# Three score tiles and a single bank for bites in late attention; experts' tiles in pairs with shared array rows

## The chip, the cores and the metric

The kernel runs on one core of one Trainium2 chip, as one program that computes a whole transformer block. The metric is the device time of one execution in microseconds. The program has in-order engines that run side by side: PE (TensorE, with PEld for its weight loads), ACT (ScalarE), DVE (VectorE), POOL (GpSimd), and SP (SyncE), which issues most DMAs. Matrix products land in PSUM, which has eight banks of 128 x 512 float32. Everything here is float32. A float32 matmul shows as two PE instructions, and a transpose against the identity as one.

## The reference

The input is x[4, 1024, 256]; every position t of the second axis has four rows, one for each l.

```
x = x + attention(layernorm(x))     # 16 heads of 16, rotary, per-head layernorm of q and k,
                                    # scores ** 4, causal mask, divided by their sum, then w_out
x = x + ffn(layernorm(x))
x = x + conv(layernorm(x))          # a convolution over the first axis (4 taps), then silu
x = x + ffn(layernorm(x))

def ffn(x):                         # 4096 rows of 256
    shared = silu(x @ s1_gate) * (x @ s1_up) @ s2          # width 352
    probs = softmax(x @ gate_w.T)                          # 16 experts
    weights, chosen = top_k(probs, 6)
    for each row and each chosen expert e:
        h = silu(x @ w1[e]_gate) * (x @ w1[e]_up)          # width 176
        out += weight * (h @ w2[e])                        # 176 x 256
    return out + shared
```

The hidden width of an expert, 176, is 128 + 48, so the contraction of the second matmul (the down projection) takes two weight loads of at most 128 rows.

## The kernel before

**Attention.** A pass is half hf of the 1024 positions, times a pair u (one of four l and one of two groups of heads): eight passes with hf = 0 (early) and eight with hf = 1 (late). A step (n, a, j) of a pass handles one block j of 128 keys for four heads. An early pass has 2 x 4 steps and a late one 2 x 8, so there are 64 early and 128 late steps. `forward` calls `scores`, two steps ahead (LOOK = 2): four matmuls of 32 contraction rows each (L694), one for each head, into two score tiles of 128 x 2 x 512 (two banks each); ACT squares both from PSUM (L705); then masks (DVE L712, POOL L714); then the second square, of tile 0 on DVE (L725), of tile 1 on ACT (L863, in the next turn of the loop) or in part on POOL. `weigh` (L742) multiplies with v into the one accumulator bank. PSUM there: a pool of two score tiles (four banks), one accumulator, three banks for everything else ("m").

That everything else is cut into bites: generators that yield "pe", "el" or "gap", in five lanes of the class `Bites`: QKV0, QKV1 (projection, rotary, norms and transposes of a coming pass: `qkv_bites`, started by `begin_chain`), NORM, OUT (collecting a pass's output and projecting it), and ROUTE (taps, zero fill of the queues xq, then for the first half of the rows the router: `prepare`, `plan`, `scatter`). `bites.step(pe, counts)` runs up to counts[lane] bites of each lane in the order of the lanes, and at most pe bites of kind "pe" over all of them. There are two such calls in a step. `plan` computes the slots of all rows in queues sorted by expert, and a table of the expert of each of 111 tiles of 128 slots. `scatter` normalizes two 128-row blocks into a buffer sxn (two buffers, DVE L200) and sends them to xq in DRAM with 12 indirect DMAs from POOL (L421), 96 in all.

The order of instructions on PE, DVE, ACT and SP is the order of the program text; POOL's is the compiler's.

**Feed-forward.** `stream` runs 4 stages of 111 tiles: stage 0 and 2 for the first and second feed-forward of the first half of the rows, 1 and 3 for the other half. Iteration c does `load` (SP, three tiles a DMA, xg), `gate_up(c)` (L1030, weights picked by a register; Silu on ACT L1038, product on DVE L1039 into hbuf), `turn_h(c - 2)` (two transposes of hbuf, L1044, copied by ACT to hT), `turn(c + 2)` (two transposes of the tile's input, L1014), `down(c - 3)` (L1053: hT's first 128 rows with w2a and the rest, 48 rows padded with zeros to 128, with w2b; copied by ACT to yo, stored by SP to yq for every third tile), and then the stage's own function, which runs bites in three lanes: QUEUE (`combine` of the stage before: gathers from yq by indirect DMAs on POOL, L1147, added into X on DVE, L1131; then `fill`, the scatter for the stage after), SIDE (`convolve`, `prepare`, `plan`) and FILL (`shared`, the shared expert: L955, L972). If the next stage's queue is not filled six tiles before it is wanted, `force` runs what is left of the lanes at once. After the last tile the rest of `combine` runs with `shared` of the last half.

All weights of the experts lie in SBUF: wgu, w2a, and w2b with all 16 experts.

## Time and profile before

| | |
|---|---|
| median of 3 runs | 2390.59 us (2389.18 to 2391.22) |
| the profiled execution | 2393.24 us, its span 2391.5 us |
| busy, PE / PEld | 2114.5 us (88%) / 1308.4 us (55%) |
| busy, DVE / ACT / POOL | 1118.5 / 1240.2 / 901.4 us (47, 52, 38%) |
| mean granted PE clock | 0.925 |
| early attention; late attention | to 275.2 us; 275.2 to 760 us |
| first gate_up of stages 0 to 3 | 854.8, 1168.9, 1570.8, 1977.0 us |
| last gate_up; end | 2253.7 us; 2391.5 us |
| scatters, gathers on POOL (L421, L1147) | 384 x 0.987 us, 384 x 0.979 us |
| chain that ended last, by engine | PE 67%, DVE 12%, issue 7%, ACT 7%, POOL 5%, DMA 2% |

Matmuls are pipelined and their ends are modelled, so a busy PE is read by the distances between starts. In a line of the timeline the columns are start, duration, engine, line, operation, out<-in, shape and count, and in brackets the idle time of the engine just before and what ended it. Idle time of an engine that does not set the end costs nothing.

### The profile page before, as it was taken

What the parts mean: (1) busy time and instruction counts of PE and PEld (TensorE: products, weight loads), DVE (VectorE), ACT (ScalarE), POOL (GpSimd) and SP (SyncE); (2) the same over time, 40 slices, a digit from 0 to 9 for tenths busy, and PEclk for the clock granted to TensorE, in tenths of its full rate; (3) what the DMA queues carried; (4) which work ended last, traced back from release to release, by engine and by line L of the source; (5) the groups of instructions that cost most, each with busy time, mean ns of one, the idle gap of its engine ahead of it and who ended that gap; (6) DMA issues with size and microseconds to landing.
All of it is one profiled execution on the core that took longest, in us unless ns stands there. A gap on an engine that the chain in (4) does not pass through costs nothing.

```text
span 2391.5 us, 33033 instructions
## 1 busy us (share of the span) xinstructions
PE 2114.5 (88%) x10480; PEld 1308.4 (55%) x10480; DVE 1118.5 (47%) x2532; ACT 1240.2 (52%) x2754; POOL 901.4 (38%) x990
## 2 busy tenths in 40 slices
PE   5899999778898998999899999789999959999974
PEld 2344443222233466777666667567676747777632
DVE  5888867656555225111166652126754212441154
ACT  3677878566676145555455544335553424555410
POOL 3333211344431000444355226645513654540176
PEclk8888988889888999999999999989999979999987
DMA  7900000111101412555455335344423535663243
GB/s 232 342 7 1 1 1 1 38 51 45 53 27 62 114 48 79 165 166 166 137 151 154 102 104 176 132 139 142 145 92 121 176 124 154 202 186 115 91 123 112
DMA packets 212231, 267.73 MB, mean 112 GB/s; under 512 B 25280, under 2 KB 187232, under 8 KB 212064
## 3 DMA queue, kind: packets, MB, share of 16 engines
q1 hardware_dynamic: 166944, 161.04, 21.6%
q0 software_dynamic: 36992, 100.78, 13.4%
q10 hardware_dynamic: 8128, 3.80, 0.7%
q8 instruction: 91, 1.49, 0.3%
q14 instruction: 76, 0.62, 0.1%
HBM read 123.72 MB, written 141.82 MB: 111 GB/s over the span
## 4 chain that ended last, share of the span: by engine, by line
PE 67%; DVE 12%; issue 7%; ACT 7%; POOL 5%; DMA 2%; ACTq 0%; POOLq 0%; DVEq 0%; SPq 0%
PE pgu L1030 20%; PE py L1053 14%; PE ps L694 6%; PE acc L742 4%; PE pxt L1014 4%; PE pht L1044 4%; POOL xq L421 3%; PE pg L955 3%; ACT s L705 3%; PE pj L571 3%; PE pu L955 3%; PE po L972 3%; POOL yg L1147 2%; ACT s L863 1%; DVE X L1131 1%
## 5 line engine op out<-in xcount | busy, mean ns | idle before, releaser
L421 POOL DMA_INDIRECT xq<-sxn,sloti x384 | 379.2, 987 | 644.7 <-ACT xgT L1016 306.2
L1030 PE MATMUL pgu<-wgu,xgT 128*128 x1776 | 609.7, 466 | 4.4 <-DVE hbuf L1039 2.2
L1147 POOL DMA_INDIRECT yg<-yq,sloti x384 | 375.8, 979 | 421.8 <-issue 201.4
L1039 DVE TENSOR_TENSOR hbuf<-hbuf,pgu 128x176 f32<-128x176 f32 x444 | 149.4, 337 | 721.7 <-ACT hbuf L1038 721.2
L1030 PEld LDWEIGHTS pgu<-wgu,xgT 128*128 128x128 f32 x1776 | 338.7, 193 | 136.5 <-issue 20.3
L1038 ACT ACTIVATE hbuf<-pgu 128x176 f32<-128x176 f32 x444 | 141.4, 318 | 411.7 <-PE pgu L1030 411.6
L705 ACT ACTIVATE s<-ps 128x1024 f32<-128x1024 f32 (+3 forms) x384 | 291.4, 815 | 114.6 <-PE ps L694 113.5
L1053 PE MATMUL py<-w2a,hT 128*128 x888 | 268.7, 385 | 0.9 <-ACT yo L1062 0.9
L1053 PE MATMUL py<-w2b,hT 128*128 x888 | 266.4, 382 | 0.0
L1062 ACT COPY yo<-py 128x256 f32<-128x256 f32 x444 | 166.1, 374 | 167.0 <-PE py L1053 166.7
L1131 DVE SCALAR_TENSOR_TENSOR X<-yg,top,X 128x256 f32<-128x256 f32 x384 | 186.0, 484 | 87.8 <-DMA yg<-yq,sloti 81.8
L1014 PE MATMUL pxt<-ident,xg 128*128 128x128 f32 x888 | 171.8, 276 | 60.6 <-DMA xg<-xq 60.6
L714 POOL TENSOR_SCALAR_AFFINE_SELECT s<-s 128x256 f32<-128x256 f32 x128 | 84.2, 659 | 349.7 <-ACT s L705 349.5
L725 DVE TENSOR_TENSOR s<-s 128x1024 f32<-128x1024 f32 (+3 forms) x160 | 168.2, 1051 | 86.8 <-ACT s L705 83.5
L1016 ACT COPY xgT<-pxt 128x256 f32<-128x256 f32 x444 | 167.9, 378 | 68.7 <-PE pxt L1014 68.3
L694 PE MATMUL ps<-q,kA 32*128 32x512 f32 (+3 forms) x1024 | 182.0, 647 | 20.0 <-ACT s L705 18.0
L1044 PEld LDWEIGHTS pht<-ident,hbuf 128*128 128x128 f32 x888 | 125.9, 142 | 124.4 <-issue 71.1
L1053 PEld LDWEIGHTS py<-w2b,hT 128*128 128x128 f32 x888 | 170.2, 192 | 23.5
L863 ACT ACTIVATE s<-s 128x1024 f32<-128x1024 f32 x192 | 164.4, 856 | 27.5 <-POOL s L714 27.2
L1044 PE MATMUL pht<-ident,hbuf 128*128 128x128 f32 x888 | 171.6, 275 | 4.9 <-ACT hT L1046 4.9
L1046 ACT COPY hT<-pht 128x256 f32<-128x256 f32 x444 | 165.4, 372 | 1.7 <-PE pxt L1014 0.7
L742 PE MATMUL acc<-s,vA 128*32 128x512 f32 (+3 forms) x1024 | 140.1, 603 | 13.2 <-ACT s L863 10.8
(158 smaller groups left out, 2421.9 us busy)
## 6 DMA issues: line engine op xcount, KB each, us to landing
xg<-xq SPq DMA_DIRECT2D x148, 384.0 KB, 3.7
yq<-yo SPq DMA_DIRECT2D x148, 384.0 KB, 2.8
xq<-zero SPq DMA_DIRECT2D x74, 384.0 KB, 4.6
xq<-sxn,sloti POOLq DMA_INDIRECT x384, 2.4
yg<-yq,sloti POOLq DMA_INDIRECT x384, 2.9
wgu<-in_w SPq DMA_DIRECT2D x4, 1408.0 KB, 17.8
X<-in_x SPq DMA_DIRECT2D x8, 512.0 KB, 5.5
out<-X SPq DMA_DIRECT2D x8, 512.0 KB, 3.5
```

Of the source, the lines that this page charges most:

```text
L421: d = nc.gpsimd.indirect_dma_start(out=xq[g][:, :], out_offset=bass.IndirectOffsetOnAxis(ap=sloti[:, c + i, k : k + 1], axis=0), in_=xs[:, ...
L694: nc.tensor.matmul(tiles[h // 2][:, h % 2, 0:nq], lhsT=kt[32 * h : 32 * h + 32, (j % 4) * P : (j % 4 + 1) * P], rhs=qT[u, hf][a][32 * h : ...
L705: nc.scalar.activation(s2[:, :, 0:nq], tiles[pr][:, :, 0:nq], AF.Square)
L725: nc.vector.tensor_mul(part, part, part)
L742: nc.tensor.matmul(acc[32 * r : 32 * r + 32, n0:512], lhsT=va[:, j % 4, h * VW : h * VW + 32], rhs=s2s[r // 2][:, r % 2, 0 : 512 - n0], st ...
L863: nc.scalar.activation(part, part, AF.Square)
L1014: nc.tensor.transpose(pt[:, k, :], xg[c][:, k * P : (k + 1) * P], ident)
L1030: nc.tensor.matmul(pg, lhsT=xT[c][:, k, :], rhs=wgu_f[k][:, bass.ds(vals[0] * (2 * FI), 2 * FI)], start=(k == 0), stop=(k == 1),)
L1044: nc.tensor.transpose(pt[:, k, :], hbuf[c % 4][:, k * P : (k + 1) * P], ident)
L1053: nc.tensor.matmul(py, lhsT=hT[c][:, k, :], rhs=w2_f[k][:, bass.ds(off[c] * E, E)], start=(k == 0), stop=(k == 1),)
L1131: nc.vector.scalar_tensor_tensor(X[:, t, l, :], yg[:, k, :], top[:, i, k0 + k : k0 + k + 1], X[:, t, l, :], op0=ALU.mult, op1=ALU.add,)
L1147: nc.gpsimd.indirect_dma_start(out=yg[:, k, :], out_offset=None, in_=yq[g][:, :], in_offset=bass.IndirectOffsetOnAxis(ap=sloti[:, i, k0 + ...
```

## The change

In attention the PSUM pools go. There are now three score tiles (six banks), one bank `sums` for the accumulator and one bank `spare`. Early passes use two score tiles and turn `spare` and the two banks of the third tile over to the bites; late passes use all three score tiles in turn, and their bites have `spare` alone and run "pe" bites only in the second `bites.step` of a step, one at most. In late passes DVE also takes the second square of tile 1 at j = 1 and 3. Chains of late passes begin two passes ahead (at a = 1, j = 6), with a third vB buffer.

In the stream, tiles go in pairs. The pair's hidden rows lie in one buffer of 3 x 128 columns, the even tile's 176 from the left, the odd tile's 176 from the right, so that the middle 128 columns hold the even tile's last 48 and the odd tile's first 48, and one transpose turns both. `down` runs once a pair: for each tile a matmul with 128 rows of its expert (w2a in two layouts), then for each a matmul with its half of the middle (64 rows of the array, with 48 that are not zero). The 48 rows of w2 for each tile are no longer held for all experts but fetched by SP with a DMA for each tile (`fetch`), by a register that SP loads from the table. yo is copied and stored once a pair.

The lanes run otherwise too: middle stages take 1 + i % 2 bites of QUEUE and 3 of SIDE an iteration (1 and 2 before); `final` takes one of QUEUE each time with two gathers a bite (every second time with three before); `combine` keeps three bites pending, in four buffers yg; `plan` compares in chunks of 19 tiles (six bites) instead of 37 (three).

The diff, cut to its core:

```diff
-        for c in range(0, NTILE, 37):
+        for c in range(0, NTILE, 19):
+            n = min(19, NTILE - c)
             yield "el"
...
-        vB = [v_buffer(f"vB{i}") for i in range(2)]
+        vB = [v_buffer(f"vB{i}") for i in range(3)]
...
+        score_tiles = [pp.tile([P, 2, 512], FP, name=f"sc{i}") for i in range(3)]
+        sums = pp.tile([P, 512], FP, name="sums")
+        spare = pp.tile([P, 512], FP, name="spare")
...
+        early = Banks([spare, score_tiles[2][:, 0, :], score_tiles[2][:, 1, :]])
+        late = Banks([spare])
+        PS = {"m": early}
+        turn = [0]
...
-            tiles = [PS["s"].tile([P, 2, 512], FP, tag="s", name="ps") for _ in range(2)]
+            tiles = []
+            for _ in range(2):
+                tiles.append(score_tiles[turn[0] % (2 if hf == 0 else 3)])
+                turn[0] += 1
...
-                if pr == 0 and (hf == 1 or j % 2 == 0):
+                if pr == 0 and (hf == 1 or j % 2 == 0) or hf == 1 and j in (1, 3):
                     nc.vector.tensor_mul(part, part, part)
...
-            if hf == 1 and u > 0 and a == 0 and j == 3 and n + 1 < len(passes):
-                begin_chain(n + 1)
+            if hf == 1 and a == 1 and j == 6 and n + 2 < len(passes):
+                begin_chain(n + 2)
+            if hf == 1:
+                PS["m"] = late
...
-                    bites.step(1, (1, 1, 1, 1, 1))
+                bites.step(0 if PS["m"] is late else 1, (1, 1, 1, 1, 1))
...
-        w2b = fw.tile([P, NEXP, E], FP, name="w2b")
-        nc.vector.memset(w2b[32:64], 0.0)
-        nc.vector.memset(w2b[64:P], 0.0)
-        nc.scalar.dma_start(out=w2b[0:FB], in_=w2r[P:FI])
+        w2a = []
+        for a in range(2):
+            w2a.append(fw.tile([P, NEXP, E], FP, name=f"w2a{a}"))
+            nc.scalar.dma_start(out=w2a[a], in_=w2r[a * FB : a * FB + P])
+        w2b = [fw.tile([P, E], FP, name=f"w2b{i}") for i in range(3)]
+        for w in w2b:
+            nc.vector.memset(w, 0.0)
...
+            def fetch(c):
+                _, vals = expert(c, SP)
+                if tiles[c][1] % 2 == 0:
+                    rows, src = slice(0, FB), bass.ds(vals[0] * FI + P, FB)
+                else:
+                    rows, src = slice(P - FB, P), bass.ds(vals[0] * FI, FB)
+                nc.sync.dma_start(out=w2b[nth_pair(c) % 3][rows, :], in_=w2[src, :])
...
             def turn_h(c):
                 pt = ps_t.tile([P, 2, P], FP, tag="t", name="pht")
-                for k in range(2):
-                    nc.tensor.transpose(pt[:, k, :], hbuf[c % 4][:, k * P : (k + 1) * P], ident)
+                c0 = 2 * P * (tiles[c][1] % 2)
+                nc.tensor.transpose(pt[:, 0, :], pair(c)[:, c0 : c0 + P], ident)
+                if ends_pair(c):
+                    nc.tensor.transpose(pt[:, 1, :], pair(c)[:, P : 2 * P], ident)
...
+                py = ps_y.tile([P, 2, 512], FP, name="py")
+                for a in range(n):
+                    nc.tensor.matmul(
+                        py[:, a, 0:E],
+                        lhsT=hT[c + 1 - n + a][:, 0, :],
+                        rhs=w2a_f[a][:, bass.ds(off[c + 1 - n + a] * E, E)],
+                        start=True,
+                        stop=False,
+                    )
+                for a in range(n):
+                    rows = slice(HP * a, HP * a + HP)
+                    nc.tensor.matmul(
+                        py[:, a, 0:E],
+                        lhsT=hT[c][rows, 1, :],
+                        rhs=w2b[nth_pair(c) % 3][rows, :],
+                        start=False,
+                        stop=True,
                     )
+                yo = f2.tile([P, 2, E], FP, name="yo")
+                nc.scalar.copy(yo[:, 0:n, :], py[:, 0:n, 0:E])
...
                 if c >= 3:
-                    down(c - 3)
+                    if ends_pair(c - 3):
+                        down(c - 3)
+                if c + 2 < n:
+                    fetch(c + 2)
...
-                    yg = f3.tile([P, n, E], FP, tag="yg", name="yg")
+                    yg = f4.tile([P, n, E], FP, tag="yg", name="yg")
...
-                    if len(pending) > 2:
+                    if len(pending) > 3:
...
-                bites.step(1, (1, 2, 0))
+                bites.step(1, (1 + i % 2, 3, 0))
...
-                bites.add(QUEUE, combine(0, 3, store))
-            bites.step(1, (1 if i % 2 == 0 else 0, 0, 0))
+                bites.add(QUEUE, combine(0, 2, store))
+            bites.step(1, (1, 0, 0))
...
-            bites.add(QUEUE, combine(1, 3, last))
+            bites.add(QUEUE, combine(1, 2, last))
```

`prepare` and `plan` in the stream take their PSUM from the two banks of `shared`, since `py` now takes two.

## The prediction

> **What bounds the kernel now.** I read the windows by stage first, then the chain of waits, then the timeline inside each stage. Late attention (the passes with hf = 1, 275 to 760 us) in the windows, then the waits in it (who waited for whom: total us, times, longest):
>
> ```profile
> 275.20:760.00 484.80, 416.20 (x2484) 146.06 (x2483) 297.56 (x535) 353.97 (x484) 148.97 (x173) 0.87 0.08 27
> ...
> PEld ps L694 <- ACT s L705: 111.5, 132, 2.1
> ...
> ACT s L705 <- PE ps L694: 79.9, 72, 3.3
> ...
> ACT s L863 <- POOL s L714: 27.2, 8, 8.3
> ```
>
> (The last line is from the same query over 440 to 765 us.) After the span the columns are PE, PEld, DVE, ACT, POOL, clock. Nothing is full: ACT works 354 of 485 us, and it waits 80 us for scores while the scores wait 111 us for ACT's squares: a ping-pong over two score tiles, at a clock of 0.87.
>
> The tile stream, one iteration of the timeline on PE, undisturbed:
>
> ```profile
> 1000.85 1.35 PE L1030 MATMUL pgu<-wgu,xgT 128*128 x4
> ...
> 1002.04 0.38 PE L1044 MATMUL pht<-ident,hbuf 128*128 128x128 f32 x2
> ...
> 1002.25 0.38 PE L1014 MATMUL pxt<-ident,xg 128*128 128x128 f32 x2
> ...
> 1002.47 0.60 PE L1053 MATMUL py<-w2a,hT 128*128 x2
> ...
> 1002.91 0.59 PE L1053 MATMUL py<-w2b,hT 128*128 x2
> ...
> 1003.34 1.35 PE L1030 MATMUL pgu<-wgu,xgT 128*128 x4
> ```
>
> Starts tell the price, because ends overlap: gate and up 1.19 us, transposes 0.21 a pair, each half of down 0.435; 2.49 in all, with no idle. The stream is bound by PE, except at the borders between stages:
>
> ```profile
> 1555.97 0.96 POOL L421 DMA_INDIRECT xq<-sxn,sloti  x1 [0.30 <-issue]
> 1557.24 0.96 POOL L421 DMA_INDIRECT xq<-sxn,sloti  x1 [0.30 <-issue]
> 1558.51 0.96 POOL L421 DMA_INDIRECT xq<-sxn,sloti  x1 [0.31 <-issue]
> 1560.97 0.89 SPq L1001 DMA_DIRECT2D xg<-xq  x2
> ...
> 1564.44 0.66 PE L1014 MATMUL pxt<-ident,xg 128*128 128x128 f32 x2 [25.68 <-DMA xg<-xq]
> ```
>
> An indirect DMA occupies POOL for 0.96 + 0.30 = 1.267 us (gathers 1.253), and PE idled 25.7 us because the scatter for the next stage was not issued in time. The tail (2264 to 2385) is 96 gathers at 1.253, bound by POOL.
>
> **What a change of array tiling costs.** PE in late attention alternates full-array and row-tiled work:
>
> ```profile
> 604.45 1.56 PE L571 MATMUL pj<-wqkv_sb,xnT 128*128 128x384 f32 x4
> 605.93 1.14 PE L694 MATMUL ps<-q,kB 32*128 32x512 f32 x8
> 607.00 1.56 PE L571 MATMUL pj<-wqkv_sb,xnT 128*128 128x384 f32 x4
> ```
>
> From gate and up, a pass costs 1.19 / (4 x 352) = 0.845 ns a column. Four passes of 384 should take 1.30; pj takes 1.48. The eight score passes, four row groups side by side, are two passes deep: 2 x 512 x 0.845 = 0.87; they take 1.07. So sharing of rows is real, and each switch of tiling costs about 0.2 us.
>
> **The change, part by part.**
>
> *Pairs of experts.* Per pair one transpose goes (0.107 us), and the four w2b passes (0.87 us) become two passes side by side: 2 x 256 x 0.845 = 0.43, plus a switch in and one out, 0.40: 0.84. Gain 0.03 + 0.107 = 0.137 us a pair; 220 pairs: 30 us. The bounds: switches free, 0.54 a pair; passes not overlapping at all, 0.87 + 0.40, a loss of 0.29 a pair. I take the middle because the score lines show both the sharing and the switch.
> The Trainium skill, TensorEngine Tiling (Array Packing), Tiling Modes, says that changing the mode drains TensorE, and its table of theoretical speedup promises up to 2x for a contraction of 64. By that table alone the pair would gain 0.43 in the second matmuls, some 96 us in all; the rows above say that the drain eats nearly all of it.
>
> ACT's copies: one 128x512 (o_sb, 0.59) in place of two of 0.374, hidden. SP: per pair one store, two register loads and two w2b fetches of 48 KB in place of 0.67 stores. A DMA issue is 0.36 us there, so with the register loads some 2 us per 4.8. Each fetch sits behind the store, which waits for ACT's yo copy; behind it wait the next xg load and the next store. It lands some 3 to 4 us later (xg median 3.7), and its matmul comes three iterations (7 us) after issue. Cover enough; without it 3 us a pair. The extra 22 MB are small against the 135 GB/s already moving. Also gone is the w2b memset (3.5 us) that held up ACT's first hxT copy: 2 us.
>
> *Lanes in the stream.* I counted the bites by iteration from the step counts in the code. For before, this leaves 3 scatters at the first border and 16 at each of the next two; the trace shows just that. After: combine in middle stages runs over iterations 0 to 31 (was 0 to 47), the scatter over 45 to 77 (was 66 on), so both middle borders lose their stall: 25.7 plus some 1.3 at half clock, 2 x 27 = 54 us gained. The first border gets 6 scatters instead of 3, because plan has three more bites: +4 us.
> But 1.5 bites of two DMAs an iteration ask POOL for 3 x 1.26 = 3.8 us, and PE needs 2.42 plus about 0.8 of shared and prepare. The 48 combine bites take POOL 120 us and 12 to start, against some 113 on PE; DVE waits for yg in order, and the product for hbuf behind it on DVE stalls PE. After four buffers of slack, 10 to 14 us. The scatter: 122 against about 100, with slack of a chunk of 12: 7. Three SIDE bites an iteration crowd DVE too, and prepare now shares two banks with shared, so some of its twelve PE bites a stage wait for a product (0.68) on DVE. I take 20 us a middle stage (bounds 0 and 40): +40. Final: 2.51 on POOL against 2.42: +3. Tail: POOL's 96 gathers stay, 8 rows in flight instead of 9: 0.
>
> *Late attention.* With three tiles the first of the next scores waits for the first square, not the second: 0.97 us earlier for each of 72 waits, at most 70 us; I take 40, since PE also takes its bites there. 32 squares of 1.0 us leave ACT: 354 to 322. DVE gets 32 x 1.23 = 39 us on 298; it is in order and feeds the sums, so +15 comes back. The rest of ACT's idle (131 - 80 = 51: POOL's selects, the square root behind DVE) stays. 322 + 40 + 51 + 15 = 428; 485 - 428, rounded down, gives 55. Bounds: 15 (PE with one bank per step is the next limit: its bites, about 14 a pass, now fill nearly every step and each waits for the copy of the one before) and 95. The chains begin 18 steps ahead instead of 13 (vB has a third buffer for that); by my count no bite has to be forced at the start of a late pass, before or after: 0. Early attention has the same three banks: 0.
>
> *Scatter at the end of attention.* One PE bite per step starves ROUTE, the last lane: plan ends at step 143 instead of 105, and the scatter starts at step 145 of 192 instead of 107, with 25 of 96 DMAs left after the last step. The trace shows POOL sending each chunk of 12 at once when its sxn is there; sxn of the seventh chunk comes two steps before the end, so 24 x 1.267 + 2.4 = 33 us run from about then, against 6 us of projection left. The semaphore waits ahead of the first hxn in the trace take in every lane that scatters report on, and the FFN's first work on DVE, ACT, SP and PE is behind it. So +27 us of idle PE (bounds 0 and 33).
>
> **The sum.** The profiled execution took 2393.24 (span 2391.5), 2.65 above the median. -55 + 27 - 30 - 54 + 4 + 40 + 3 - 2 = -67: 2326, or 2324 as a median.
>
> **Rivals.**
> 1. *Switches are cheap for two halves of the array* (0.17): pairs gain 0.54, another 90 us of PE time. For it: only the way into 32-row tiles was seen. Against it: the score rows. In middle stages POOL keeps about half of each from using it, so some 55 more: 2269.
> 2. *Late attention stays as it is* (0.13): bites on one bank and DVE's extra squares replace the wait for ACT. For it: PE at 86% busy and DVE's order. 2324 + 55 = 2379.
> 3. *Slower: the second matmuls do not overlap* (0.12). Two halves of 64 rows run one after the other, 0.87 + 0.40 against 0.87, and PE is the bound: 0.43 worse a pair than forecast, 95 us, of which POOL's lag gives back 15: 2404. It decides once the excursion takes over 1.14 us instead of 0.84 (67 / 220 more a pair). Against it: eight score passes in 1.07.
>
> **Numbers.** Forecast 0.58 with its own range 2285 to 2372; rivals 0.17, 0.13, 0.12. 0.2% is about 5 us, what a measurement of this kernel can tell. Faster: 0.58 + 0.17 + most of 0.13 = 0.85; same 0.03; slower 0.12. The range leaves out the lower half of rival 1 and rival 3: 2264 to 2388.
>
> **What would show it.** Right: the start of pgu every 2.4 us on the mean of two tiles, the w2b passes starting in twos and the next pgu 0.84 us after them; no border idle over 10 us but the first; DVE waiting for yg in the middle stages; PE idle some 25 us ahead of the first hpt with POOL scattering; ACT's wait for ps halved. Wrong: the excursion at 0.45 or 1.2 us, late attention still 480 us, or scatters that end before the last step.

## The result: 1.4% slower

The changed kernel takes 2424.76 us (median of four runs, 2418.00 to 2431.53); the kernel before, run beside it, 2390.90. The ratio is 1.0142, with a 95% interval of 1.0111 to 1.0172: some 34 us lost where 67 were forecast to be gained, and outside the forecast range. The profiled execution after took 2431.53 us (span 2429.8) against 2393.24 (span 2391.5) before, so the two traces differ by 38.3 us, and that is the difference which is taken apart here. The sections are cut at the same events in both traces: ScalarE's first Square of scores, its 16th and 32nd copy to `o_sb` (end of early and of late attention), the first gate and up of each stage, the last one, the end.

| Section | before, us | after, us | change | forecast |
|---|---|---|---|---|
| up to the first Square | 35.8 | 36.8 | +1.0 | 0 |
| early attention | 245.3 | 271.2 | **+25.9** | 0 |
| late attention | 479.5 | 446.2 | -33.3 | -55 |
| from there to the first tile's gate and up | 94.2 | 115.8 | +21.6 | +25 |
| first stage | 314.1 | 306.8 | -7.3 | -3.5 |
| the two middle stages | 808.1 | 834.9 | **+26.8** | -29 |
| final stage | 276.7 | 274.7 | -2.0 | -4.5 |
| tail | 137.8 | 143.5 | +5.7 | 0 |

The end of early attention lies 6 us later here (281.1 us before) than where the table ahead of the prediction has it (275.2), so late attention before is 479.5 us here and 484.8 there. The sum of the changes is 38.4 us. Against the forecast, 56 us are missing in the middle stages, 26 in early attention, 22 in late attention and 6 in the tail.

What the forecast got right can be read first. The steady pair, TensorE's timeline after (start, duration, instruction):

```profile
1100.56 1.35 PE L1089 MATMUL pgu<-wgu,xgT 128*128 x4
1101.75 0.27 PE L1104 MATMUL pht<-ident,hbuf 128*128 128x128 f32 x1
1101.86 0.38 PE L1071 MATMUL pxt<-ident,xg 128*128 128x128 f32 x2
1102.07 1.03 PE L1118 MATMUL py<-w2a,hT 128*128 x4
1103.03 0.70 PE L1127 MATMUL py<-w2b,hT 64*128 64x256 f32 x4
1103.66 1.45 PE L1089 MATMUL pgu<-wgu,xgT 128*128 x4
1104.95 0.27 PE L1104 MATMUL pht<-ident,hbuf 128*128 128x128 f32 x1
```

From the first w2a pass to the next gate and up are 1.59 us; 0.87 of them are w2a's own (4 x 256 x 0.845 ns), 0.72 the excursion to w2b, and that gate and up then takes 1.29 to the next transpose instead of 1.19. Together 0.82, where 0.84 were forecast. The w2b passes start in twos (1103.03 and 1103.04, 1103.35 and 1103.36), and gate and up starts come at 3.11 and 1.72 us in turn: 4.83 a pair where two single tiles took 4.97. That is 0.14 us a pair, as forecast. The Trainium skill, TensorEngine Tiling (Array Packing), Theoretical Speedup, gives up to a factor of two for a contraction of 64; the estimate by it for the w2b passes is 0.43 instead of 0.87. They came at 0.72, and the next gate and up is 0.10 longer. The same page says, under Tiling Modes, that a change of mode drains TensorE; an extra 0.39 us around these passes agrees with that, though the trace shows no drain as such.

The middle border, after:

```profile
1586.49 0.38 PE L1071 MATMUL pxt<-ident,xg 128*128 128x128 f32 x2
1586.71 1.35 PE L1089 MATMUL pgu<-wgu,xgT 128*128 x4
1588.00 0.38 PE L1071 MATMUL pxt<-ident,xg 128*128 128x128 f32 x2
1589.81 1.45 PE L1089 MATMUL pgu<-wgu,xgT 128*128 x4
```

The start of gate and up at 1589.81 is the next stage's first tile, and it follows without a stall: the 25.7 us of idle time are gone, as forecast. The end of attention, after, also went as forecast; POOL still scatters when the projection is over, and TensorE waits 20 us for it:

```profile
784.00 0.96 POOL L424 DMA_INDIRECT xq<-sxn,sloti  x1 [0.30 <-issue]
789.14 2.24 PE L184 MATMUL hpt<-ident,hxn 128*128 128x128 f32 x8 [20.37 <-DVE hxn L202]
```

In the tail POOL's gathers now wait for VectorE, which has to be done with a row buffer before it is filled again. The wait (total us, times, longest) before, then after:

```profile
POOL yg L1147 <- DVE X L1131: 2.1, 7, 0.3
```

```profile
POOL yg L1219 <- DVE X L1203: 13.1, 22, 1.9
```

Now the middle stages. The windows by stage (span, then busy time of PE, PEld, DVE, ACT, POOL, clock, DMA), first before:

```profile
1168.90:1570.80 401.90, 362.96 (x1645) 264.50 (x1645) 176.46 (x472) 187.67 (x503) 189.01 (x192) 0.95 0.44 136
1570.80:1977.00 406.20, 367.30 (x1658) 267.82 (x1657) 177.35 (x473) 187.83 (x503) 189.43 (x192) 0.95 0.43 135
```

and after:

```profile
1176.80:1589.80 413.00, 369.11 (x1591) 234.91 (x1589) 177.87 (x478) 170.33 (x448) 191.34 (x192) 0.93 0.47 146
1589.80:2011.70 421.90, 377.22 (x1604) 239.61 (x1602) 178.34 (x479) 170.22 (x448) 189.62 (x192) 0.92 0.46 143
```

TensorE has as much idle time as before (44 against 39 us), though the border stall is gone, and its busy time grew by 6 where fewer passes should have cut it by 7.6: the granted clock fell from 0.95 to 0.93. So the idle time moved into the stage, and the clock is lower with it. What TensorE waits for in the first of these windows (total us, times, longest), before for the copy of `hT`, then after:

```profile
PE pht L1044 <- ACT hT L1046: 2.2, 2, 1.8
```

```profile
PE pht L1104 <- ACT hT L1109: 16.4, 7, 5.0
PE pgu L1089 <- DVE hbuf L1098: 14.9, 8, 4.4
PE pa L346 <- DVE mask L339: 7.5, 1, 7.5
```

How the longest of the first kind comes about, the timeline after shows (ScalarE, VectorE and TensorE; in brackets the idle time before the instruction and what ended it):

```profile
1219.11 0.48 DVE L1203 SCALAR_TENSOR_TENSOR X<-yg,top,X 128x256 f32<-128x256 f32 x1 [3.33 <-DMA yg<-yq,sloti]
...
1222.08 1.40 DVE L192 BATCH_NORM_STATS2 ln_st<-X 128x6 f32<-128x256 f32 x4
...
1223.80 0.30 ACT L197 ACTIVATE c_rstd<-c_mv,eps_t 128x4 f32<-128x4 f32 x1 [6.73 <-DVE c_mv L194]
...
1226.10 0.38 ACT L1109 COPY hT<-pht 128x256 f32<-128x256 f32 x1
...
1226.53 0.48 PE L1104 MATMUL pht<-ident,hbuf 128*128 128x128 f32 x1 [4.99 <-ACT hT L1109]
```

Read from the bottom up: TensorE waits 5 us for ScalarE's copy of `hT`; ScalarE has stood 6.7 us at a square root of `convolve`, which a SIDE bite put ahead of that copy; the square root waits for VectorE's statistics, and VectorE had been waiting for a gathered row and then had four more to add. One late row of `combine` goes through two engines that work in order and stops the third, which works for another tile. The forecast had this chain with VectorE alone (the product for `hbuf` behind the row, 14.9 us of the wait lines); it did not have ScalarE in it (16.4).

### The profile page after: what moved, and what is told of

It reads as the page before. It is cut to its first block, busy times and chain, and to the rows that moved or that the text cites. A ratio compares the mean times of both kernels' runs of the same rounds, so it can differ in the third digit from the quotient of the medians.

```text
span 2429.8 us, 34168 instructions
## 1 busy us (share of the span) xinstructions
PE 2043.0 (84%) x10260; PEld 1157.9 (48%) x10260; DVE 1149.8 (47%) x2588; ACT 1139.7 (47%) x2502; POOL 921.8 (38%) x991
## 3 DMA queue, kind: packets, MB, share of 16 engines
q1 hardware_dynamic: 196576, 182.89, 24.3%
## 4 chain that ended last, share of the span: by engine, by line
PE 44%; DVE 7%; DMA 6%; POOL 4%; issue 4%; ACT 2%; SPq 0%; POOLq 0%; DVEq 0%; ACTq 0%
PE pgu L1089 18%; PE py L1118 6%; PE py L1127 4%; DMA yg<-yq,sloti 3%; PE pg L988 3%; PE pxt L1071 3%; POOL yg L1219 3%; PE po L1005 3%; PE pu L988 3%; DMA xq<-sxn,sloti 2%; DVE X L1203 2%; POOL xq L424 1%; PE pht L1104 1%; PE pl L291 1%; PE fpt L184 1%
## 5 line engine op out<-in xcount | busy, mean ns | idle before, releaser
L740 ACT ACTIVATE s<-sc 128x1024 f32<-128x1024 f32 (+3 forms) x384 | 291.2, 815 | 115.4 <-PE sc L729 114.7
L1135 ACT COPY yo<-py 128x512 f32<-128x512 f32 x224 | 130.7, 583 | 243.3 <-PE py L1127 243.3
L760 DVE TENSOR_TENSOR s<-s 128x1024 f32<-128x1024 f32 (+1 forms) x192 | 201.6, 1064 | 71.2 <-ACT s L740 67.9
L1071 PE MATMUL pxt<-ident,xg 128*128 128x128 f32 x888 | 174.0, 279 | 13.3 <-DMA xg<-xq 13.3
L1127 PE MATMUL py<-w2b,hT 64*128 64x256 f32 x888 | 162.8, 441 | 5.6 <-DMA w2b<-in_w 5.6
L1118 PEld LDWEIGHTS py<-w2a,hT 128*128 128x128 f32 x888 | 155.8, 196 | 13.9 <-ACT yo L1135 1.5
L773 PE MATMUL sums<-s,vA 128*32 128x512 f32 (+3 forms) x1024 | 129.2, 562 | 38.3 <-ACT o_sb L782 14.0
L729 PE MATMUL sc<-q,kA 32*128 32x512 f32 (+3 forms) x1024 | 133.6, 588 | 17.8 <-ACT s L740 13.3
L1109 ACT COPY hT<-pht 128x128 f32<-128x128 f32 (+1 forms) x444 | 140.5, 317 | 1.7 <-PE pht L1106 1.2
L893 ACT ACTIVATE s<-s 128x1024 f32<-128x1024 f32 (+3 forms) x160 | 128.9, 806 | 16.3 <-POOL s L749 16.2
L1071 PEld LDWEIGHTS pxt<-ident,xg 128*128 128x128 f32 x888 | 112.6, 143 | 48.3 <-issue 46.1
```

What stands on the lines that cost most here:

```text
L740: nc.scalar.activation(s2[:, :, 0:nq], tiles[pr][:, :, 0:nq], AF.Square)
L760: nc.vector.tensor_mul(part, part, part)
L1071: nc.tensor.transpose(pt[:, k, :], xg[c][:, k * P : (k + 1) * P], ident)
L1118: nc.tensor.matmul(py[:, a, 0:E], lhsT=hT[c + 1 - n + a][:, 0, :], rhs=w2a_f[a][:, bass.ds(off[c + 1 - n + a] * E, E)], start=True, stop=F ...
L1127: nc.tensor.matmul(py[:, a, 0:E], lhsT=hT[c][rows, 1, :], rhs=w2b[nth_pair(c) % 3][rows, :], start=False, stop=True,)
```

## Experiments

The first group ran on a chip like that of the comparison (the kernel before: 2392.83 us). All later groups ran on two others, where the kernel before takes 2472 to 2478 us; what differs there is told at the end, and until then those runs are read by sections, one against another. The expected totals of the later groups were mostly worked out from the first chip, and most of them missed.

### Which bites stall the middle stages

Four kernels that differ from the changed one only in the step of the middle stages:

```
lanes_1_2    bites.step(1, (1, 2, 0))
lanes_15_2   bites.step(1, (1 + i % 2, 2, 0))
lanes_1_3    bites.step(1, (1, 3, 0))
lanes_split  bites.step(1, (1 + i % 2 if st in scattering else 1, 2, 0))
             # scattering: the stages whose fill(st + 1) has been added
```

> The changed kernel with the middle stages' bites back at one QUEUE bite and two SIDE bites per tile. Theory A (combine at 1.5 bites per tile is what stalls the middle stages) and theory B (three SIDE bites per tile are what stalls them) both expect: the iterations of 10 to 17 us go, the border stalls of about 30 us come back (22 DMAs are left at each border by a count of the bites), middle stages about 402 and 406 us instead of 413 and 422, and some 2398 us in all instead of 2425. Theory C (neither; the pairs themselves, their fetches, or prepare and shared on two common banks, cost the time) expects the long iterations to stay and the border stalls on top: middle stages about 440 us, 2475 us in all.

> The changed kernel with two SIDE bites per tile instead of three, QUEUE as changed (1 + i % 2). Theory A (combine's rate): the long iterations stay, 2425 us within 8. Theory B (three SIDE bites): middle stages shorter by about 20 us each, 2385 us. Theory C: as A, 2425.

> The changed kernel with one QUEUE bite per tile, SIDE at three as changed. Theory A (combine's rate): long iterations gone, 10 DMAs left at each border, so a border stall of about 18 us; middle stages about 388 us each, 2366 us in all. Theory B (three SIDE bites): the long iterations stay, with the border stall on top, 2440 us. Theory C: 2450.

> The changed kernel with one QUEUE bite per tile while combine runs and 1 + i % 2 only for the scatter of the next stage, SIDE at two. Theories A and B both expect no long iterations in the first half of a middle stage and no border stall (the count leaves no DMA at the border): middle stages about 370 us, 2331 us in all. Theory C: 2425 or more. A fourth possibility, that the faster scatter costs what the border stall did because its row copies on VectorE wait for GpSimd: middle stages about 395, 2385.

Measured: 2429.67, 2424.35, 2425.97 and 2390.11 us; ratios to before 1.0159 [1.0141, 1.0178], 1.0137 [1.0115, 1.0159], 1.0146 [1.0128, 1.0164] and 0.9986 [0.9973, 0.9998]. By stretches of a middle stage, the mean of the two, from the starts of gate and up:

| | tiles 0-47 | 48-68 | 69-108 | the border (109, 110) | whole stage |
|---|---|---|---|---|---|
| before | 165.0 | 80.1 | 125.3 | 33.6 | 404.1 |
| lanes_1_2 | 174.7 | 81.8 | 122.3 | 40.8 | 419.6 |
| lanes_1_3 | 181.7 | 88.7 | 122.3 | 24.3 | 416.9 |
| lanes_split | 175.2 | 82.2 | 129.9 | 12.3 | 399.6 |
| lanes_15_2 | 204.4 | 72.9 | 135.4 | 4.7 | 417.3 |
| after | 213.7 | 73.0 | 126.2 | 4.7 | 417.5 |

What follows, step by step, for tiles 0 to 108 (before 370.5; 363 due with the gain of the pairs):

- *Combine at 1.5 bites a tile costs 25 us a stage* (lanes_15_2 412.6 against lanes_split 387.2). The changed kernel has several iterations of 10 to 18 us in each middle stage; with one bite a tile the longest is 8.6 (lanes_1_2). Theory A holds for the iterations; its totals were wrong. The path of the stop varies with the bites: in lanes_15_2, as slow as the changed kernel, TensorE waits only 6.3 us for `hT` in the first of these stages, but 21.3 for the router's rows `rxn` from VectorE, behind the rows of `combine` and another of ScalarE's square roots.
- *The third SIDE bite costs nothing at that rate* (after 412.8 against 412.6), and 14 us at one bite a tile (lanes_1_3 392.6 against lanes_1_2 378.7; one iteration of 12.6 is there), which its earlier scatter gives back at the border. Theory B falls as the cause of the loss.
- *The denser scatter costs 8.5 us* (387.2 against 378.7) *and takes away 28* (the border). The forecast said 7 and 27. The fourth possibility of lanes_split came nearest in its numbers (2385 us, stages of 395), but not for its reason: the scatter costs less than a third of what the border did.
- *16 us remain with the old bites* (lanes_1_2 378.7 against 363): none of the theories had that, and its 2398 us came out as 2430. All of it lies ahead of tile 69, where `combine`, `convolve`, `prepare` and `plan` run; tiles 69 to 108, with the scatter, are 3.0 us shorter than before, as is due. The next group asks for it.

The denser scatter's price has a line in lanes_split. VectorE, timeline of that run:

```profile
1503.52 0.78 DVE L202 TENSOR_SCALAR sxn<-X,mvs,rstds 128x256 f32<-128x256 f32 x2 [8.62 <-DMA xq<-sxn,sloti]
1504.22 0.57 DVE L1098 TENSOR_TENSOR hbuf<-hbuf,pgu 128x176 f32<-128x176 f32 x2
...
1504.60 1.45 PE L1089 MATMUL pgu<-wgu,xgT 128*128 x4 [2.73 <-DVE hbuf L1098]
```

The copy of rows waits until the scatter of the chunk before has left its buffer, two products for `hbuf` wait behind it, and TensorE for them.

### What remains with the old bites

Tiles 0 to 108 of the first and of the second middle stage, before:

```profile
1168.92:1537.19 368.27, 355.01 (x1621) 258.82 (x1620) 175.09 (x469) 185.22 (x496) 173.62 (x176) 0.99 0.45 140
1570.84:1943.38 372.54, 359.27 (x1634) 262.13 (x1633) 175.99 (x470) 185.38 (x496) 174.03 (x176) 0.98 0.45 139
```

and in lanes_1_2:

```profile
1171.65:1548.29 376.64, 355.05 (x1568) 225.36 (x1567) 175.03 (x473) 167.79 (x442) 168.50 (x170) 0.97 0.48 149
1588.42:1969.24 380.82, 356.86 (x1580) 227.22 (x1579) 175.47 (x474) 167.70 (x442) 168.95 (x170) 0.98 0.47 148
```

TensorE idles 21.6 and 24.0 us instead of 13.3 and 13.3: 8 and 11 of the 16 us. Its busy time is 355.1 and 356.9 where 7.6 less than before was due, 347.4 and 351.7; that is the rest. The granted clock can be a part of it: 0.97 instead of 0.99 in the first stage, and 2% of 355 is 7 us; but in the second it is 0.98 in both kernels, and 5 us stay without a cause. After single stops the clock differs. The four passes of gate and up took 2.15 us after an idle time of 2.32, at a granted clock of 0.64 (at 1208.52 in the changed kernel; 1.35 undisturbed), but 1.45 after one of 2.73, at 1.00 (at 1504.60 in lanes_split). The Trainium skill, TensorE: Matmul & The Clock Gate, HAM oscillation, warns of idle gaps above some 3.4 us. By these two rows a shorter gap can go with a lower clock too, and the length of one gap alone does not tell. TensorE's largest wait in lanes_1_2 over the first window (total us, times, longest):

```profile
PE pht L1104 <- ACT hT L1109: 9.4, 8, 2.0
```

Before, the same wait has 2.2 us. So some 7 of the 8 us of new idle time in that stage are waits for ScalarE's copy. Two causes were thought of: the two banks that `prepare` now shares with `shared`, and the pairs' uneven iterations.

```
banks_shared (the kernel before)        even_pairs (best_two_ref, see below)
-  ps_m2 = ... bufs=1 ...                - w2a of both tiles after the odd tile
-  return ps_m2                          + w2a of the even tile one iteration
+  return ps_s                           +   earlier, into the same py
```

> The kernel before, with one edit: the fifth pool of the expert part (the one bank of prepare and plan) is gone, and prepare and plan take turns with shared on shared's two banks, as in the changed kernel. One QUEUE and two SIDE bites a tile, no pairs. In the run with the old bites (lanes_1_2) a middle stage without its border took 382 us where 365 were due, 17 too many. Theory J (the shared banks cost it): each middle stage here is longer than before by 15 to 17 us, ratio to before 1.013. Theory K (the pairs cost it: after a pair's long iteration comes one of 1.72 us, and every hold-up of ScalarE longer than that stops TensorE, where 2.49 us were free before): each middle stage within 3 us of before, ratio 1.000 to 1.003.

> As best_two_ref, with the first matmul of each pair's down (w2a of the even tile) moved one iteration ahead, so that iterations of 3.11 and 1.72 us become some 2.7 and 2.15. Theory K (a hold-up of ScalarE beyond 1.72 us stops TensorE in the paired stream): each middle stage 5 to 10 us shorter than in best_two_ref, first and last stage the same within 2. Rival: the single py tile is asked for one iteration earlier and waits for ScalarE's copy of the pair before; every iteration pays some 0.1 to 0.5 us and the whole is 20 to 100 us longer.

banks_shared: ratio 1.0011 [0.9992, 1.0029]. The shared banks cost nothing on that chip, where theory J asked for 1.013; it falls. even_pairs: iterations of 2.67 and 2.16, ratio 1.0039 [1.0017, 1.0060] against 1.0060 [1.0038, 1.0082] for its yardstick, two intervals that overlap; in one trace of each the middle stages are 2.6 and 3.9 us shorter, the final one 1.7, while the new wait for the copy to `yo` ahead of w2a adds up to 34 us over the kernel on TensorE's weight loads. Theory K has the right sign and about half of the size it expected; if it holds, the unevenness is some 3 of the 16 us. What the rest hangs on was not separated: lanes_1_2 also differs from the kernel before in the fetches, in the buffers of `combine` and in the chunks of `plan`. On the other chips the 16 us do not show at all (below).

### Early attention: two banks that count as one

```
- score_tiles = [... for i in range(3)]            # each [P, 2, 512]
+ score_tiles = [... for i in range(2)]
+ third = [pp.tile([P, 512], ...) for i in range(2)]
- early = Banks([spare, score_tiles[2][:, 0, :], score_tiles[2][:, 1, :]])
+ early = Banks([spare] + third)
  # late passes: the third tile squared by two instructions of 512 columns
```

> The changed kernel with the third score tile as two tiles of one bank each, so that the early passes have three separate banks for bites; in the late passes that tile is squared by two instructions of 512 columns instead of one of 1024. Theory D (the two halves of one score tile are treated as one: the second user waits for the last reader of the first): early passes back to about 240 us from 265, late passes up to 5 us longer for the extra instructions, 2404 us in all. Rival E (the early loss comes from elsewhere, such as the order of bites or the static score tiles): early passes stay at about 265, 2425 to 2430 us.

> The changed kernel's expert part with the attention part of the kernel before (pools of score tiles, three banks for bites, one Square on ScalarE for the odd steps). If the parts add up: gate and up of the first tile starts at about 855 us instead of 870, and the whole takes 2425 - 15 = 2410 us. If the attention part's change is worth what it gains in the late passes alone (35 us), which the trace of the changed kernel speaks against: 2460 us.

In the changed kernel, at the end of early attention:

```profile
270.17 0.68 DVE L833 TENSOR_TENSOR X<-X,sc 128x512 f32<-128x512 f32 x1
270.90 3.45 PE L825 MATMUL sc<-wout_sb,aT 128*128 128x256 f32 x8 [3.77 <-DVE X L833]
```

The second projection goes to the other half of `sc`, a bank of its own, and yet starts only when VectorE has read the first. Early attention took 271.2 us in the changed kernel and 269.0 to 273.6 in all six experiments that keep its banks (269.0 and 273.6 on the chip of early_apart); with the halves as tiles of their own it took 252.7 in early_apart and 247.9 to 254.6 in the eight later kernels built like it, 247.8 with the attention of before. Theory D holds: 19 of the 26 us. The late passes took 453.5, 7 more than in the changed kernel, where up to 5 were expected. The Trainium skill, Perfetto Trace Analysis, Optimizing Tensor Performance, advises that independent matmul groups rotate through different PSUM banks; here that was so on paper only: the groups had three banks, and two of them, as halves of one tile, waited as one.

attn_before (ratio 1.0545 [1.0514, 1.0577]) came out slower than early_apart (1.0455 [1.0421, 1.0489]): early 247.8, but late 503.4. Its 2410 us was written for the first chip and can't be held against this one, nor can the 2404 of early_apart: both keep the changed kernel's step, whose first 48 tiles of a middle stage take 235 us here and 214 there.

### Late attention and the scatter at its end

```
late_act_sq     - if pr == 0 and (hf == 1 or j % 2 == 0) or hf == 1 and j in (1, 3):
                + if pr == 0 and (hf == 1 or j % 2 == 0):
late_two_bites  - bites.step(0 if PS["m"] is late else 1, (1, 1, 1, 1, 1))
                + bites.step(1, (1, 1, 1, 1, 1))
```

> The changed kernel without the 32 extra squares on VectorE (steps j = 1 and 3 of the late passes go back to ScalarE). Theory F (late passes are held by VectorE's order: squares behind plan, rotary and norm): late passes shorter by 10 to 15 us, 2412 us. Rival G (ScalarE is still the bound): late passes longer by about 20 us, 2445 us.

> The changed kernel with two TensorE bites allowed per late step instead of one. Theory H (the budget of one starves the last lane, so plan and scatter come late): scatter starts some 100 us earlier and is over before the last step, idle time before the first hpt about 27 us shorter, but the late passes themselves longer by about 10 to 20 us since two bites share one bank: 2410 us. Rival: the second bite in a step waits for the copy of the first and late attention gives back all of it: 2430 to 2440 us.

They measured 1.0517 [1.0490, 1.0545] and 1.0525 [1.0497, 1.0553]. Neither has a yardstick on that chip, since the changed kernel itself was not run there. So both edits were made again on a kernel with the other repairs:

```
best          early_apart and lanes_split; combine in bites of one row, two a tile
              (eight buffers), three bites a step in the tail
best_two      best with the edit of late_two_bites
best_act_sq   best with the edit of late_act_sq
```

> The changed kernel with three repairs: the third score tile as two tiles of one bank (as in early_apart), combine at two rows a tile and the next stage's scatter at 1 + i % 2 bites of two (as in lanes_split), and combine in bites of one row over eight row buffers in place of bites of two over four, with three such bites per step in the tail. If the repairs add up: early passes 252 us instead of 271 (-18), late passes +5, middle stages -35 in all, tail 138 us instead of 144 (-6): 2370 us, ratio to before 0.991. If the tail's 6 us come from the order of shared's work and not from the grain of the bites: 2377. If bites of one row load VectorE's order more than those of two: middle stages no shorter than in the changed kernel, 2400.

> As best, with two TensorE bites allowed per late step instead of one. In the run late_two_bites the late passes took 457 us and the idle time to the first tile's gate and up fell to 98. Theory H: late passes 10 us longer than in best, the way from the last late step to the first tile 18 us shorter: 8 us faster than best. Rival: no gain, within 3 us of best.

> As best, with the 32 squares back on ScalarE. Theory F (VectorE's order holds the late passes): late passes 10 us shorter than in best. Rival G (ScalarE is the bound): 15 to 20 us longer. If both limits are near each other: within 5 us of best.

Ratios: 1.0072 [1.0050, 1.0095], 1.0035 [1.0011, 1.0059], 1.0078 [1.0051, 1.0105]. A second TensorE bite a step lengthens the late passes by 1.7 us (454.8 against 453.1), and the way to the first tile falls from 115.6 to 95.3 us: theory H holds, 18.6 us by these sections, 11 in the medians. In best 23 of the 96 scatters are left after the end of late attention, in best_two none. The budget of one bite, not the three score tiles, put the scatter at the end. Giving the 32 squares back to ScalarE shortens the late passes by 7.4 us and lengthens the way to the first tile by 4.7; the first gate and up starts at 853.6 against 853.1, after an early attention 3.7 us longer in that trace. If that is more than scatter between traces, both limits are near each other; the same late passes as in best_two took 458.0 to 464.4 us in four other traces. As for the totals, best was expected at a ratio of 0.991 and came out above 1.

That VectorE's order holds up the sums at times, the changed kernel's timeline shows:

```profile
536.06 2.73 DVE L339 TENSOR_REDUCE mask<-hot 128x256 f32<-128x1536 f32 x1
...
538.72 2.55 DVE L760 TENSOR_TENSOR s<-s 128x1024 f32<-128x1024 f32 x2
...
541.33 1.94 PE L773 MATMUL sums<-s,vA 128*32 128x512 f32 x8 [3.91 <-DVE s L760]
```

Two squares stand behind a reduction of `plan`, and the sums behind them. Of the ping-pong that the third tile was to end, one half went: the score matmuls wait 41 us for the squares instead of 110. The other half, ScalarE's wait for scores, fell only from 79 to 58. The waits of late attention after (308 to 754 us):

```profile
ACT s L740 <- PE sc L729: 57.9, 59, 5.7
PEld sc L729 <- ACT s L740: 41.0, 61, 1.7
ACT s L893 <- POOL s L749: 16.2, 6, 4.8
```

### Two other chips, and versions without pairs

```
best_two_ref     the kernel of best_two, as yardstick
yo_three         yo in three buffers, six row buffers of combine
before_split     the kernel before with lanes_split's step for the scatter
no_pairs         before_split behind the attention of best_two
pairs_same_chip  the kernel of even_pairs, beside these two
```

> The kernel of the run best_two (three separate early banks, two late TensorE bites, combine at two rows a tile, bites of one row), here as the yardstick of the next two. Where VectorE and ScalarE wait for nothing that the profile shows in the middle stages (87 such waits of VectorE for 143 us in best_two, 1 to 3 us in the changed kernel's own trace), it stays slower than before, ratio 1.0035. Where they do not, the sum of the repairs is due: early passes -18, drain -18, middle stages -35, tail -6 against the changed kernel, 2425 - 77 = 2348, ratio 0.982.

> As best_two_ref, with three buffers of yo instead of two and six row buffers of combine instead of eight. Theory L (ScalarE's copies to yo wait for the store of two pairs ago, which lands late behind fetches of w2b): where such waits show (80 us in best_two), middle and final stages shorter by 20 us or more in all; where they don't, within 4 us of best_two_ref. Rival M (ScalarE's idle time there is not a wait for a store): no difference in either case.

> The kernel before with one edit of the changed kernel's idea alone: the next stage's scatter runs at 1 + i % 2 bites of two a tile, combine stays at one. By a count of the bites no DMA is left at a middle border. Theory (the border stall is worth its idle time, less what a denser scatter holds up VectorE's row copies): two borders x (28 - 8) us = 40 us gained, ratio 0.983. Rival: the scatter's hold-ups give back what the border had cost, as far as the stage's end goes: within 5 us of before, ratio 0.998 to 1.002.

> The expert part of before_split, without pairs, behind the attention part of best_two (three separate early banks, three score tiles, one late bank with two TensorE bites a step). In best_two the first gate and up came at 838 us where the kernel before has 855; so 12 to 17 us faster than before_split: ratio 0.977, if the two halves add up. If the gain of the late passes depends on the chip: ratio 0.983 to 0.99.

> The kernel of even_pairs, beside the two without pairs, on one chip. What the pairs are worth by themselves: the steady iteration says 0.14 us a pair, 30 us for the whole, faster than no_pairs. The middle stages of lanes_1_2 say that hold-ups of ScalarE and the lower clock after them give back 15 to 18 us in each of two stages: 0 to 5 us slower than no_pairs. Where VectorE and ScalarE have long waits without a cause in the profile (the last two groups of runs): 60 us slower or more.

Ratios: 1.0060 [1.0038, 1.0082], 1.0089 [1.0060, 1.0119]; 1.0095 [1.0081, 1.0110], 1.0138 [1.0118, 1.0159], 1.0039 [1.0026, 1.0053]. yo_three is slower where theory L expected 20 us of gain. The waits ahead of `yo` that it was to take away (79 us in both) did not change. It also has two row buffers fewer, and its loss sits in the tiles where `combine` runs: tiles 0 to 47 of a middle stage take 185.2 us instead of 175.2, the others the same within 2. So the buffers are the likely cause, and theory L was not tested by itself.

On these chips VectorE and ScalarE have long waits for which the profile shows no cause. VectorE's wait ahead of the product for `hbuf` (total us, times, longest), in best_two_ref, in banks_shared, which is nearly the kernel before, and in lanes_split on the first chip:

```profile
DVE hbuf L1108 <- issue: 177.1, 97, 5.2
```

```profile
DVE hbuf L1038 <- issue: 74.5, 48, 6.1
```

```profile
DVE hbuf L1098 <- issue: 1.8, 3, 0.8
```

The long iterations lie where POOL sends its indirect DMAs; that these are the cause is not shown. Tiles 69 to 108 with the denser scatter take 130 us in lanes_split on the first chip; here they take 171 in before_split, 173 in no_pairs and 169 to 173 in the paired kernels with that scatter, but 130 at one bite a tile (banks_shared). So here the denser scatter costs some 41 us a stage, and the border that it takes away 28 (32.7 to 5.0). In all, the two middle stages of before_split are 16.5 us longer than those of banks_shared; its median is 23.8 us above the kernel before, where 40 of gain were expected. no_pairs, expected at 0.977 to 0.99, missed with it.

The expert part (first gate and up to the end) takes 6.7 us longer with pairs than without (pairs_same_chip 1644.3, no_pairs 1637.6): first stage -7.3, middle stages -5.1 and -9.7, final stage +32.5, tail -3.9. But these two do not differ in the pairs alone. In the final stage pairs_same_chip gathers two rows a tile in bites of one, no_pairs three rows every second tile, and the loss lies where those gathers run: tiles 0 to 63 take 203 us against 168, and after them 16 tiles take 38.6 against 39.8, the steady gain of the pairs. So the +32.5 is no price of pairs that these runs show, and that the 0 to 5 us of the expectation came near is luck; its 60 were wrong. In the middle stages the pairs are 7.4 us ahead on the mean, all of the 7.6 due, so the 16 us of the first chip are not seen here; `combine` runs there in bites of one row over eight buffers, and whether that or the chip makes the difference, no run separates.

That pairs_same_chip is faster in all comes from late attention, 464.4 against 492.5 us, with the same source for that part but for the chunks of `plan`. ScalarE waits 43.1 us for POOL's masks there in no_pairs and 19.8 in pairs_same_chip; what makes POOL later, no run shows.

No version beat the kernel before by more than 0.2%; lanes_split at 0.9986 is the only one below it. With early_apart and best_two it would come to an estimated 2360 on the first chip (2390 less 18.5 and 18.6, plus the late passes of best, 453 against 444 in lanes_split), but no run there shows it.

## Why the prediction was wrong, step by step

- **Pairs: -30, right.** 0.14 us a pair, first stage -7.3. "I take the middle because the score lines show both the sharing and the switch" held, and neither the cheap switch nor the slower rival came. But the 0.14 is the gain in an undisturbed stream; the step put no price on what a pair does to a disturbed one. In lanes_1_2 the paired stream lost 16 us a middle stage, a loss that the other chips do not show and that no run pins on the pairs.
- **Middle borders: -54, right** (33.6 to 4.7 us each).
- **Middle stages: "I take 20 us a middle stage (bounds 0 and 40)", the term that failed.** It is 48 on the mean (before 404.1 less 7.6 and 27 against 417.5), above its own upper bound. By the experiments: combine 25 where 10 to 14 were said, the scatter 8.5 where 7 were said, the paired stream 16 where nothing was said. The step took combine's cost from POOL's lag, with VectorE's order alone between the rows and TensorE. Missing were ScalarE as a second engine in order behind VectorE (TensorE's wait for `hT`, 16.4 us instead of 2.2), and the lower clock (0.93 instead of 0.95 over the stage).
- **Early attention: "the same three banks: 0", wrong by 26.** The count of banks was right and the tiles were not looked at: two of the three banks were halves of one tile, which early_apart prices at 19 us. The rest, some 7 us, is not explained.
- **Late attention: -55, came out -33**, inside its bounds of 15 to 95. ScalarE's busy time is 317 (322 forecast); its idle time is 129 instead of the forecast's 106. The mis-sized term is "I take 40" for the wait for scores, which only fell by 21: "ACT's wait for ps halved" did not come, 79 to 58 us, and 18 of the 23 us lie there. The waits of the score matmuls for the squares fell from 110 to 41.
- **Scatter at the end: +27 less 2, came out +21.6.** Right: 23 DMAs were left after the last step where 25 were counted, and best_two shows the cause.
- **Tail: 0, came out +5.7.** The gathers took 126.4 us from first to last instead of 119.8. "8 rows in flight instead of 9: 0" was the error: less the 0.30 us that stand ahead of every gather, POOL's 22 waits for VectorE's products are 6.5 us, the whole of it. The finer bites of best, with eight rows as well, did not shorten the tail on their chip (153.4, against 151.1 to 153.7 with bites of two).
- **The slower rival was another one.** It was put at second matmuls that do not overlap; the loss came from bites and banks, with the overlap as forecast. That bites at 1.5 a tile stop TensorE stood only inside a term with a bound of 40, and had no chance of its own.

## What to carry to other kernels

A stall at a border is one stop and is paid once; before spreading its work over the stage, follow each spread bite through every engine that takes its instructions in order, and look at the granted clock of the stage as well. Count dependencies by tiles and not by banks: two halves of one tile may wait as one, as they did here. When a budget is cut, look at the lane that is served last, and repair one lane at a time: here the scatter alone took the gain, while combine at the same rate gave it back.

## What the runs showed that was not expected

The same kernel takes 2391 to 2393 us on chips like the first and 2472 to 2478 on two others. There, with no more than its banks shared, it has 74 us of waits ahead of one VectorE instruction for which the profile names no cause, and a paired version has 177; before_split gained nothing although lanes_split gained 20 us a stage from the same step on the first chip. And stops come with a lower clock: in the changed kernel's middle stages TensorE idles 5 and 6 us more than before, border included, at a granted clock of 0.93 and 0.92 instead of 0.95, and its busy time rose by 6 and 10 us although fewer passes should have cut it by 7.6.
